# Retention and FFN on one core: the order of work in block 0's FFN, one tile's home, the order of products, one search operation

## The chip, the cores and the metric

The kernel runs on one core of a Trainium2 chip. A core has five engines with an instruction queue each: TensorE (PE: matmuls, with its weight loads listed apart as PEld), VectorE (DVE), ScalarE (ACT), GpSimd (POOL) and SyncE (SP), which here only issues DMAs. They work from SBUF, a memory of 128 partitions, and from PSUM, where matmuls accumulate. The metric is device time in microseconds (us).

## The reference, cut to what matters

x is 4 sequences of 1024 tokens, 512 wide, all fp32. Two sublayers follow each other, each with a plain layer norm before it and after it:

```python
x = x + layernorm(retention(layernorm(x)))
x = x + layernorm(ffn(layernorm(x)))

def retention(x):
    q, v = x @ Wq.T, x @ Wv.T
    ret = scan(v)                      # state = lam * state + v, along a sequence; one lam per head of 32
    y = layernorm(q * ret) * gamma + beta
    return (y * silu(x @ Wg.T)) @ Wo.T

def ffn(x):
    # each weight is rounded to fp8 (e4m3) and used in fp32; each product is scaled per output column
    gate = silu(qmm(x, gate_w, gate_scale))      # 512 -> 1536
    up = qmm(x, up_w, up_scale)                  # 512 -> 1536
    return qmm(gate * up, down_w, down_scale)    # 1536 -> 512
```

## The kernel before, in words

**Tiling.** The 4096 tokens are 8 blocks of 512 (t = 0 to 7). The main loop goes over the blocks, and in a block over 12 steps i, one for each 128 columns of the FFN's inner width. A step of block t issues on PE `f.gate(i)` (8 matmuls into the PSUM tile pfg), parts of the retention of block t+1 (b in the code), `f.up(i)` (8 into pfu) and `f.down(i-2)` (8 into the sums pd). A step takes PE about 8.89 us. n is the retention of block t+2, whose layer norm and transposed input xnT are prepared meanwhile. pfg and pfu share a pool of two PSUM tiles, so that the matmuls of a gate need the tile that ACT read for the gate before; `f.fuse(i)` is DVE's product of gate and up (the operation gate<-pfu,us_sb,gate, called gate_i STT here), and ACT's cast of it to fp32r (fuse); `f.rest(i)` is DVE's subtraction that leaves the cast's error (the "lo" half). The down products use both halves, as gate and up use both halves of their input x1nT (`upper_of`: ACT's cast; `rest_of`: DVE's rest).

**Order.** Every engine executes its instructions in the order of the program: the wrapper `InOrder` passes each one through `keep_in_program_order`, and all instructions therefore carry its line, L74, in the profile. The order is written out by hand. A wait at the head of an engine's queue holds all that is behind it.

**Block 0.** The FFN weights are rounded to fp8's grid while the loop's block 0 already runs, in pieces of 128x1024: `rounds` issues DVE's parts (a bitwise and on scr, an addition scr+scr, a subtraction into gate_sb, up_sb or down_sb), `units` ACT's two operations on scr between them. The squares' weights get sums on DVE (`weight_sums`) that are stored to DRAM by SP (`keep_sums`).

**Block 1's retention**, in block 0's loop, is done with plain matmuls. Its layer norm over y sums on PE: `halves()` splits a sum into hi (ACT) and lo (DVE), `mean()` and `var()` multiply both by a constant matrix. `center_y()` is four DVE subtractions y-mu, four ACT squares, and three POOL additions sqsum<-sqsum,sq. `silu(c)` puts the gate g_c into a tile with the tag "sg", of which three exist and which the FFN's gates use too.

**Blocks 2 to 7's retention** (`FAST = 2`) computes v, q and g with seven products of half size each (Strassen's way, in Winograd's form), in the order of the list `order`. Product j takes one of four sums of xnT's quarters, made by POOL (`input_sums`, t_sums), and a weight piece that SP fetches into a ring of four (`fetch_weights`, w_ring). Products 1, 2, 3 and 5 accumulate in the PSUM tile bank_a (5 begins it anew), 6, 7 and 4 in bank_b:

```python
if j == 1:
    act.copy(p1, bank)                              # p1 is a slice of the tile mids
elif j == 6:
    dve.tensor_tensor(c12, bank, p1, ALU.add)
elif j == 7:
    dve.tensor_tensor(s167, bank, p1, ALU.add)
elif j == 2:
    self.take(k, 0, 0, bank)                        # v: two scans on DVE
```

The first three products of v for block t+2 are issued in step 11 of block t.

**x1n, the FFN's input.** The layer norm of block t+1's x1 is made per 128 tokens s in steps 8 to 11: x1n_s (`x1n_of`; ACT with a bias nb in blocks 0 and 1, DVE from block 2 on). For s = 0 to 2 `move_x1n` transposes it by way of DRAM: a DVE transpose into xs, four stores mxs<-xs and a load x1n<-mxs on SP's queue. For s = 3 `turn_x1n` transposes it on PE (pt<-ident,x1n). In block t >= 1, step 11 ACT's order is: cast of x1n_2, cast of fuse_11, copy of product 1 into mids, cast of x1nT from pt.

**The search.** In block 1 ACT looks through the rounded weights for one beyond fp8's range: `find_over` yields 24 operations seen<-... of 128x1536. The list `look` says how many are issued in each of the 12 steps; half of them (rounded down) come behind `f.gate`, the rest near the step's end.

Of the kernel before, what the change touches and what calls it, by code (L numbers as in the profile page):

```python
# [10 lines left out]
F32 = mybir.dt.float32  # L11
I32 = mybir.dt.int32
F32R = mybir.dt.float32r
F8 = mybir.dt.float8e4
# [3 lines left out]
P = 128  # L18
# [5 lines left out]
def retention_ffn_sandwich(  # L24
# [24 lines left out]
    TB = 512  # L49
# [8 lines left out]
    big = ctx.enter_context(tc.tile_pool(name="big", bufs=1))  # L58
    work = ctx.enter_context(tc.tile_pool(name="work", bufs=2))
# [6 lines left out]
    class InOrder:  # L66
# [9 lines left out]
    pe, dve, act, pool, sp = (  # L76
        InOrder(e) for e in (nc.tensor, nc.vector, nc.scalar, nc.gpsimd, nc.sync)
    )
# [131 lines left out]
    def units():  # L210

        while open_units:
            _, c = open_units.pop(0)
            act.activation(c, c, AF.Relu, bias=neg_low)
            act.activation(c, c, AF.Identity, scale=1.5 * 2.0**20, bias=low_unit)

    def rounds(n, now=True):
        for _ in range(n):
            next(rounding, None)
            if now:  # L220
                units()

    def find_over():


        k = 0
        for j in range(4):
            for w in (gate_sb, up_sb, down_sb):
                v = w[:, ts(j, NI // 4), :] if w is down_sb else w[:, :, ts(j, I // 4)]
                for sign in (1.0, -1.0):  # L230
                    tag = "ret" if k >= 16 else "xn"
                    seen = work.tile(list(v.shape), F8, tag=tag, name=f"seen_{k}", bufs=2 if k >= 16 else 1)
                    act.activation(
                        seen, v.bitcast(F32), AF.Relu, bias=neg_max, scale=sign,
                        accum_out=over[:, k : k + 1], saturate=False,
                    )
                    k += 1
                    yield

    search = find_over()  # L240

    def pass_over():
# [54 lines left out]
    def ps_tile(name, home="pa"):  # L297
        if home == "pa":
            pa_turn[0] = 1 - pa_turn[0]
            home = f"pa{pa_turn[0]}"  # L300
        elif home[:2] == "pa":
            pa_turn[0] = int(home[2])
        return homes[home].tile([P, TB], F32, tag=home, name=name)
# [7 lines left out]
    def turn_by_blocks(dst, src, tag, name):  # L311


        t = work.tile([P, NQ, NC, Q], F32, tag=tag, name=name)
        dve.transpose(t, src.rearrange("p (c a i) -> p a c i", c=NC, a=NQ))
        m = dram.tile([P, NQ, NC, Q], F32, tag="turn", name=f"m{name}", bufs=2)
        for b in range(NQ):
            sp.dma_start(
                m[:, b].rearrange("(a i) c j -> i a (c j)", a=NQ),
                t[ts(b, Q)].rearrange("i a c j -> i a (c j)"),  # L320
            )
        sp.dma_start(dst, m)

# [4 lines left out]

    FAST = 2
    H = TB // 2
    order = [("v", j) for j in (1, 6, 2, 7, 4, 5, 3)]
    order += [("q", j) for j in (1, 6, 2, 7, 4, 5, 3)]
    order += [("g", j) for j in (1, 2, 6, 7, 4, 5, 3)]
    banks = {"v": {1: 0, 6: 1, 5: 0}, "q": {1: 1, 6: 0, 5: 1}, "g": {1: 0, 6: 0, 5: 1}}
# [23 lines left out]
    def keep_sums(k):  # L360
        for j, t in made[k].items():
            operands[k][j] = dram.tile([P, 2, H], F32, tag=f"sum_{k}{j}", name=f"dsum_{k}{j}", bufs=1)
            sp.dma_start(operands[k][j], t)
# [12 lines left out]
    class Retention:  # L376
# [89 lines left out]
        def product(self):  # L466

            k, j = order[self.made]
            n = (self.t - FAST) * len(order) + self.made
            self.made += 1  # L470
            w = w_ring[:, n % RING]
            if j in (1, 6, 5):
                bank = ps_tile(f"p{k}{j}_{self.t}", f"pa{banks[k][j]}").rearrange("p (c f) -> p c f", c=2)
                if j == 6:
                    self.bank_b = bank
                else:
                    self.bank_a = bank
            bank = self.bank_b if j in (6, 7, 4) else self.bank_a
            for o in range(2):
                out_ = bank[:, o]  # L480
                if len(self.right[j].shape) == 4:
                    out_ = out_.rearrange("p (g j) -> p g j", j=Q)
                for c in range(2):
                    pe.matmul(
                        out_, w[:, c, ts(o, P)], self.right[j][:, c],
                        start=(j in (1, 6, 5) and o == 0 and c == 0), stop=True,
                        skip_group_check=True,
                    )
            fetch_weights()
            c12, p1, s167 = (mids[:, m] for m in (1, 2, 3))  # L490
            if j == 1:
                act.copy(p1, bank)
            elif j == 6:
# [4 lines that stand above are left out]
                self.take(k, 0, 0, bank)  # L498
            elif j == 4:
                dve.tensor_tensor(p1, bank, p1, ALU.add)  # L500
                self.take(k, 1, 0, p1)
            elif j == 5:
                dve.tensor_tensor(s167, bank, s167, ALU.add)
                self.take(k, 1, 1, s167)
            else:
                dve.tensor_tensor(c12, bank, c12, ALU.add)
                self.take(k, 0, 1, c12)
# [116 lines left out]

        def silu(self, c):
            home = big if self.t == 0 and c == 3 else work
            tag = "fuse" if home is big else "sg"
            self.g[c] = home.tile([P, TB], F32, tag=tag, name=f"g_{self.t}_{c}", bufs=3)
            act.activation(self.g[c], self.pg.pop(c), AF.Silu)

        def g_of(self, c, home="pa"):
# [43 lines left out]
        def x1_moments(self, s):  # L675
            self.mvo[s] = moments(self.xt[s])

        def x1n_of(self, s):
            self.center(self.x1n[s], self.xt[s], self.mvo.pop(s))

        def new_x1nT(self):

# [9 lines left out]
        def move_x1n(self, s):  # L692

            x1n = self.x1n.pop(s)
            dst = x1n.rearrange("p (b c j) -> p b c j", b=NQ, c=NC)
            turn_by_blocks(dst, x1n, "ret", f"xs1_{self.t}_{s}")
            self.pt[s] = dst.rearrange("p b c j -> p c b j")

        def part(self, h, s):
            part = self.x1nT[:, h, :, ts(s, P)]  # L700
# [173 lines left out]
    b = Retention(1)  # L874
# [105 lines left out]

    look = [5, 5, 4, 2, 0, 0, 0, 2, 2, 2, 2, 0]
    l = None
    for t in range(NB):
        f, n = Ffn(a), None
        fast = b is not None and b.fast
        for i in range(NI):
            if t > 0 and (t > 1 or i):
                (f if i else l).rest((i - 1) % NI)  # L990
            if t == 0 and i == 0:
                n = Retention(2)
# [29 lines left out]
            if t == 0 and 8 <= i < 11:  # L1022
                for _ in range(4):
                    next(adding)
                if i == 10:
                    keep_sums("g")
            f.gate(i)
            if t == 0 and i in (5, 6):
                n.norm_x(2 * i - 10, True)
                n.norm_x(2 * i - 9, True)  # L1030
            for _ in range(look[i] // 2 if t == 1 else 0):
                next(search)

            if fast and i in (0, 1, 2, 3, 4, 5, 6):
# [12 lines left out]
                b.q(i + 2, tokens=slice(None) if i else later)  # L1047
                b.y_of(i + 2)
            if b and not fast and i == 3:
                b.halves()  # L1050
                units()
                rounds(3, now=False)
                units()
                b.g_of(0)
                b.mean()
                b.center_y()
                n.stats(3)
                n.rstd()
                n.shift()
# [14 lines left out]
                b.o(i - 7)  # L1074
            if b and i == 8:
                b.new_x1nT()
            if b and i >= 8:
                b.x1n_of(i - 8)
            if b and 8 <= i < 11:
                b.move_x1n(i - 8)  # L1080
            if b and i >= 9:
                b.upper_of(i - 9)
            if b and 7 <= i <= 10:
                b.o_moments(i - 7)
            if n and i == 11:
                n.input_sums(1, 2, 3, 4)
            units()
            f.up(i)
            f.fuse(i)
            if t == 0 and i == 4:  # L1090
                b.rstd_y()
            if n and i == 11:
                n.product()
                if t:
                    b.turn_x1n(3, "pf")
                    b.upper_of(3)
            if t == 2 and i == 0:
                next(passing)
            if fast and i < 6:
# [19 lines left out]
            if t == 0:  # L1119
                if i < 8 and i != 3:  # L1120
                    rounds(3, now=False)
                f.rest(i)
                if i < 3:
                    n.stats(i)
            for _ in range((look[i] + 1) // 2 if t == 1 else 0):
                next(search)

            if l and not b and i in (4, 5):
# [33 lines left out]
                f.down(NI - 2)  # L1162

            if t == 0 and i == 11:
                b.turn_x1n(3, "pf")
                b.upper_of(3)
                b.rest_of(3)
# [9 lines left out]
                b.var()  # L1177
                b.rstd_y()
            if n and i == 11:
                n.products(2)  # L1180
            if n and t > 0 and i == 5:
                n.stats(0)
                n.stats(1)
# [8 lines left out]
            if b and i == 4 and 0 < t < NB - 2:  # L1192
                n = Retention(t + 2)
# [4 lines left out]
        l, a, b = f, b, n  # L1198
# [68 lines left out]
```

## Time and profile before

| | |
|---|---|
| median of 3 runs | 984.25 us (983.97 to 984.66) |
| the profiled execution's own time | 983.95 us |
| its span, first to last instruction | 982.1 us |
| mean granted TensorE clock | 0.998 |
| busy: PE, PEld, DVE, ACT, POOL | 963.9, 734.3, 663.3, 369.9, 266.7 us |
| DMA | 110.07 MB, mean 112 GB/s |
| block 0's loop ends, block 1's FFN begins | about 203.3 us after the span's start |

PE's busy share by stage, from the trace cut at the blocks' borders: 194.5 of the first 203.0 us, 117.1 of the next 118.0, then 99.9% and more until 886, and 87.7 of the last 96.1. In a line of the timeline the two numbers ahead are start and busy time in us, then come the engine, the line of the code, the operation, out<-in by the program's names, the shapes, how often it was done in a row, and in brackets the idle time ahead of it and what ended that. In the waits view a line has the waiting engine and operation, whom it waited for, the total in us, how many waits, and the longest.

### The profile page before, as it was taken

To read this page: it belongs to the slowest core of one execution; us is meant where nothing else is said; L and a number is where in the kernel's file an instruction comes from. 1 tells how busy PE (TensorE), PEld (TensorE's weight loads), DVE (VectorE), ACT (ScalarE), POOL (GpSimd) and SP (SyncE) were. 2 spreads that over 40 slices of the span, in tenths; PEclk is the share of its full clock that TensorE was granted. 3 is DMA by queue.
4 is the path that set the end of the run, shared out by engine and by line. 5 is a ranking of instruction groups with operands and counts; after the bars stand their busy time and mean duration, and the time that the engine had idled before them with its cause. 6 is when DMAs were issued, how large, how long until landed. Compare 5 with 4: busy or idle time off the path is not lost.

```text
span 982.1 us, 11265 instructions
## 1 busy us (share of the span) xinstructions
PE 963.9 (98%) x3950; PEld 734.3 (75%) x3950; DVE 663.3 (68%) x1019; ACT 369.9 (38%) x556; POOL 266.7 (27%) x346
## 2 busy tenths in 40 slices
PE   9999999989999999999999999999999999999996
PEld 7456656678876888678876788768887788877885
DVE  5996979655667667675686666766667765756445
ACT  3546655467645125221432215321152211512223
POOL 1405121412324033240513305133141322322020
PEclk9999999999999999999999999999999999999999
DMA  9311413752416426253243623245241542213021
GB/s 300 119 65 65 130 63 94 228 161 75 151 53 156 128 82 225 80 143 120 86 129 93 176 77 116 87 131 151 83 150 59 135 140 76 75 37 113 1 86 43
DMA packets 90936, 110.07 MB, mean 112 GB/s; under 512 B 8064, under 2 KB 55424, under 8 KB 90880
## 3 DMA queue, kind: packets, MB, share of 16 engines
q1 hardware_dynamic: 90016, 108.70, 36.5%
q8 instruction: 31, 0.51, 0.2%
q10 hardware_dynamic: 864, 0.66, 0.2%
q14 instruction: 25, 0.20, 0.1%
HBM read 76.56 MB, written 32.77 MB: 111 GB/s over the span
## 4 chain that ended last, share of the span: by engine, by line
PE 84%; DVE 7%; ACT 4%; POOL 2%; DMA 1%; issue 1%; SPq 0%; DVEq 0%; POOLq 0%; ACTq 0%
PE pfu L74 15%; PE pfg L74 15%; PE pd L74 15%; PE pq L74 10%; PE pv L74 10%; PE po L74 9%; PE pg L74 9%; DVE scr L74 1%; DVE st L74 1%; DVE gate L74 1%; PE idle L74 1%; DVE xs L74 1%; DVE fuse L74 1%; DMA xnT<-mx 1%; POOL sqsum L74 1%
## 5 line engine op out<-in xcount | busy, mean ns | idle before, releaser
L74 PE MATMUL pfu<-x1nT,up_sb 128*128 128x512 f32 x768 | 211.5, 417 | 0.3 <-DVE gate L74 0.3
L74 PE MATMUL pfg<-x1nT,gate_sb 128*128 128x512 f32 x768 | 195.4, 396 | 1.4 <-ACT gate L74 1.4
L74 PE MATMUL pd<-down_sb,fuse 128*128 128x512 f32 x720 | 186.5, 400 | 0.0
L74 PEld LDWEIGHTS pfu<-x1nT,up_sb 128*128 128x128 f32 x768 | 144.4, 188 | 43.0 <-issue 13.4
L74 PEld LDWEIGHTS pfg<-x1nT,gate_sb 128*128 128x128 f32 x768 | 144.2, 188 | 31.7 <-ACT gate L74 1.8
L74 PEld LDWEIGHTS pd<-down_sb,fuse 128*128 128x128 f32 x720 | 134.9, 188 | 27.4
L74 ACT CAST fuse<-gate 128x512 fp32r<-128x512 f32 x90 | 55.7, 618 | 235.5 <-DVE gate L74 235.5
L74 ACT ACTIVATE gate<-pfg,gs_sb 128x512 f32<-128x512 f32 x96 | 65.7, 685 | 193.0 <-PE pfg L74 192.9
L74 DVE SCALAR_TENSOR_TENSOR gate<-pfu,us_sb,gate 128x512 f32<-128x512 f32 x96 | 71.7, 747 | 72.3 <-PE pfu L74 69.8
L74 PE MATMUL po<-wo_sb,y 128*128 128x512 f32 x256 | 114.5, 592 | 0.0
L74 POOL TENSOR_SCALAR mv<-mv 128x1 f32<-128x1 f32 (+1 forms) x82 | 19.9, 243 | 299.0 <-DVE mv L74 298.0
L74 PEld LDWEIGHTS po<-wo_sb,y 128*128 128x128 f32 x256 | 48.2, 189 | 50.3 <-issue 46.3
L74 DVE TENSOR_TENSOR fuse<-gate,fuse 128x512 fp32r<-128x512 f32 x90 | 74.5, 827 | 12.1 <-ACT fuse L74 12.1
L74 POOL TENSOR_TENSOR ysum<-y 128x256 f32<-128x256 f32 (+1 forms) x14 | 14.0, 1000 | 189.9 <-DVE y L74 189.9
L74 POOL TENSOR_TENSOR x<-x,x1n 128x512 f32<-128x512 f32 x32 | 46.8, 1463 | 45.6 <-DVE x1n L74 36.7
L74 DVE BATCH_NORM_STATS2 st<-x 128x6 f32<-128x512 f32 x64 | 43.6, 681 | 13.7 <-POOL x L74 11.3
L74 POOL TENSOR_TENSOR mv<-mv,nhalf 128x1 f32<-128x1 f32 (+1 forms) x75 | 46.3, 617 | 6.2
L74 PE MATMUL pg<-t_sums,w_ring 128*128 128x256 f32 x192 | 45.6, 380 | 0.6 <-ACT mids L74 0.6
L74 PE MATMUL pv<-t_sums,w_ring 128*128 128x256 f32 x192 | 45.4, 379 | 0.8 <-POOL t_sums L74 0.8
L74 PE MATMUL pq<-t_sums,w_ring 128*128 128x256 f32 x192 | 45.3, 379 | 0.0
L74 PEld LDWEIGHTS pg<-t_sums,w_ring 128*128 128x128 f32 x192 | 35.9, 189 | 7.3 <-ACT mids L74 2.0
L74 PEld LDWEIGHTS pv<-t_sums,w_ring 128*128 128x128 f32 x192 | 36.2, 189 | 6.6 <-POOL t_sums L74 1.0
(150 smaller groups left out, 1337.3 us busy)
## 6 DMA issues: line engine op xcount, KB each, us to landing
kept<-x SPq DMA_DIRECT2D x32, 256.0 KB, 2.1
x<-kept SPq DMA_DIRECT2D x32, 256.0 KB, 4.1
x<-in_x SPq DMA_DIRECT2D x28, 256.0 KB, 4.1
out<-d SPq DMA_DIRECT2D x27, 256.0 KB, 2.0
xnT<-mx SPq DMA_DIRECT2D x24, 256.0 KB, 4.9
w_ring<-dsum_v SPq DMA_DIRECT2D x24, 256.0 KB, 2.7
w_ring<-dsum_q SPq DMA_DIRECT2D x24, 256.0 KB, 2.6
w_ring<-dsum_g SPq DMA_DIRECT2D x24, 256.0 KB, 2.7
```

Source lines behind the costliest of these rows:

```text
L74: return lambda *args, **kwargs: tc.keep_in_program_order(op(*args, **kwargs))
```

## The change

1. **Step 3 of block 0.** `halves()` for block 1's mean moves to the end of step 2, ahead of `f.rest(2)`; the statistics of x_2 move from the end of step 2 into step 3; `g_of(0)`, `mean()` and `center_y()` now stand ahead of `rounds(3)` and the second `units()`, which stood ahead of them.
2. **Home of g_0.** Block 1's first gate gets a tile with the tag "tok" (four tiles, used by token tiles) instead of "sg".
3. **Step 11 of block 0.** Product 1 comes ahead of `f.fuse`, product 2 directly behind the down products and product 6 behind the transposes of x1n_3 (before: product 1 behind fuse, then transposes, 6, 2). x1n_3 is centred on DVE instead of ACT. The copy of product 1 of block 2's v goes to a tile of its own, and on ACT ahead of the cast of fuse_11. `turn_by_blocks` returns its final load, so that in step 10 `keep_sums("g")` stands between the stores of x1n_2 and its load. SP's order there becomes: weights of v's products 1 and 2, four stores of x1n_2, four stores of weight sums, load of x1n_2, a store of x, weights of products 6 and 7 (before: weights 1 and 6, four sums, four stores, load, store of x, weights 2 and 7).
4. **Order of v's products**, for all of blocks 2 to 7: 1, 2, 6, 7, 4, 5, 3 instead of 1, 6, 2, 7, 4, 5, 3. In step 11 of blocks 1 to 5 PE executes 1, transposes, down, 2, 6; ACT's order there stays.
5. **The search.** `look` becomes a list of pairs (behind the gate, at the end). One operation moves from the end of step 3 to the end of step 7 of block 1, and the 16th (k = 15) gets the tag "ret" instead of "xn".

The number of instructions stays the same on every engine.

```diff
--- before.py
+++ after.py
@@ -228,8 +228,8 @@
             for w in (gate_sb, up_sb, down_sb):
                 v = w[:, ts(j, NI // 4), :] if w is down_sb else w[:, :, ts(j, I // 4)]
                 for sign in (1.0, -1.0):
-                    tag = "ret" if k >= 16 else "xn"
-                    seen = work.tile(list(v.shape), F8, tag=tag, name=f"seen_{k}", bufs=2 if k >= 16 else 1)
+                    tag = "ret" if k >= 15 else "xn"
+                    seen = work.tile(list(v.shape), F8, tag=tag, name=f"seen_{k}", bufs=2 if k >= 15 else 1)
                     act.activation(
                         seen, v.bitcast(F32), AF.Relu, bias=neg_max, scale=sign,
                         accum_out=over[:, k : k + 1], saturate=False,
@@ -319,7 +319,7 @@
                 m[:, b].rearrange("(a i) c j -> i a (c j)", a=NQ),
                 t[ts(b, Q)].rearrange("i a c j -> i a (c j)"),
             )
-        sp.dma_start(dst, m)
+        return lambda: sp.dma_start(dst, m)
 
 
 
@@ -330,7 +330,7 @@
 
     FAST = 2
     H = TB // 2
-    order = [("v", j) for j in (1, 6, 2, 7, 4, 5, 3)]
+    order = [("v", j) for j in (1, 2, 6, 7, 4, 5, 3)]
     order += [("q", j) for j in (1, 6, 2, 7, 4, 5, 3)]
     order += [("g", j) for j in (1, 2, 6, 7, 4, 5, 3)]
     banks = {"v": {1: 0, 6: 1, 5: 0}, "q": {1: 1, 6: 0, 5: 1}, "g": {1: 0, 6: 0, 5: 1}}
@@ -488,6 +488,11 @@
                     )
             fetch_weights()
             c12, p1, s167 = (mids[:, m] for m in (1, 2, 3))
+            if k == "v" and self.t == FAST:
+
+                if j == 1:
+                    self.p1 = work.tile([P, 2, H], F32, tag="rstd", name="p1", bufs=1)
+                p1 = self.p1
             if j == 1:
                 act.copy(p1, bank)
             elif j == 6:
@@ -624,8 +629,8 @@
 
         def silu(self, c):
             home = big if self.t == 0 and c == 3 else work
-            tag = "fuse" if home is big else "sg"
-            self.g[c] = home.tile([P, TB], F32, tag=tag, name=f"g_{self.t}_{c}", bufs=3)
+            tag, bufs = ("fuse", 3) if home is big else ("tok", 4) if self.t == 1 and c == 0 else ("sg", 3)
+            self.g[c] = home.tile([P, TB], F32, tag=tag, name=f"g_{self.t}_{c}", bufs=bufs)
             act.activation(self.g[c], self.pg.pop(c), AF.Silu)
 
         def g_of(self, c, home="pa"):
@@ -675,8 +680,8 @@
         def x1_moments(self, s):
             self.mvo[s] = moments(self.xt[s])
 
-        def x1n_of(self, s):
-            self.center(self.x1n[s], self.xt[s], self.mvo.pop(s))
+        def x1n_of(self, s, center=None):
+            (center or self.center)(self.x1n[s], self.xt[s], self.mvo.pop(s))
 
         def new_x1nT(self):
 
@@ -693,8 +698,8 @@
 
             x1n = self.x1n.pop(s)
             dst = x1n.rearrange("p (b c j) -> p b c j", b=NQ, c=NC)
-            turn_by_blocks(dst, x1n, "ret", f"xs1_{self.t}_{s}")
             self.pt[s] = dst.rearrange("p b c j -> p c b j")
+            return turn_by_blocks(dst, x1n, "ret", f"xs1_{self.t}_{s}")
 
         def part(self, h, s):
             part = self.x1nT[:, h, :, ts(s, P)]
@@ -980,7 +985,7 @@
 
 
 
-    look = [5, 5, 4, 2, 0, 0, 0, 2, 2, 2, 2, 0]
+    look = [(2, 3), (2, 3), (2, 2), (1, 0)] + 3 * [(0, 0)] + [(1, 2)] + 3 * [(1, 1)] + [(0, 0)]
     l = None
     for t in range(NB):
         f, n = Ffn(a), None
@@ -1022,13 +1027,11 @@
             if t == 0 and 8 <= i < 11:
                 for _ in range(4):
                     next(adding)
-                if i == 10:
-                    keep_sums("g")
             f.gate(i)
             if t == 0 and i in (5, 6):
                 n.norm_x(2 * i - 10, True)
                 n.norm_x(2 * i - 9, True)
-            for _ in range(look[i] // 2 if t == 1 else 0):
+            for _ in range(look[i][0] if t == 1 else 0):
                 next(search)
 
             if fast and i in (0, 1, 2, 3, 4, 5, 6):
@@ -1047,13 +1050,13 @@
                 b.q(i + 2, tokens=slice(None) if i else later)
                 b.y_of(i + 2)
             if b and not fast and i == 3:
-                b.halves()
                 units()
-                rounds(3, now=False)
-                units()
+                n.stats(2)
                 b.g_of(0)
                 b.mean()
                 b.center_y()
+                rounds(3, now=False)
+                units()
                 n.stats(3)
                 n.rstd()
                 n.shift()
@@ -1074,26 +1077,35 @@
                 b.o(i - 7)
             if b and i == 8:
                 b.new_x1nT()
-            if b and i >= 8:
+            if b and i >= 8 and (t or i < 11):
                 b.x1n_of(i - 8)
             if b and 8 <= i < 11:
-                b.move_x1n(i - 8)
-            if b and i >= 9:
+                load = b.move_x1n(i - 8)
+                if t == 0 and i == 10:
+                    keep_sums("g")
+                load()
+            if b and i >= 9 and (t or i < 11):
                 b.upper_of(i - 9)
             if b and 7 <= i <= 10:
                 b.o_moments(i - 7)
-            if n and i == 11:
+            if n and t and i == 11:
                 n.input_sums(1, 2, 3, 4)
             units()
             f.up(i)
+            if t == 0 and i == 11:
+                n.input_sums()
+                n.product()
             f.fuse(i)
+            if t == 0 and i == 11:
+                b.x1n_of(3, center_scale)
+                n.input_sums(1, 2, 3, 4)
+                b.upper_of(2)
             if t == 0 and i == 4:
                 b.rstd_y()
-            if n and i == 11:
+            if n and t and i == 11:
                 n.product()
-                if t:
-                    b.turn_x1n(3, "pf")
-                    b.upper_of(3)
+                b.turn_x1n(3, "pf")
+                b.upper_of(3)
             if t == 2 and i == 0:
                 next(passing)
             if fast and i < 6:
@@ -1119,10 +1131,12 @@
             if t == 0:
                 if i < 8 and i != 3:
                     rounds(3, now=False)
+                if i == 2:
+                    b.halves()
                 f.rest(i)
-                if i < 3:
+                if i < 2:
                     n.stats(i)
-            for _ in range((look[i] + 1) // 2 if t == 1 else 0):
+            for _ in range(look[i][1] if t == 1 else 0):
                 next(search)
 
             if l and not b and i in (4, 5):
@@ -1162,6 +1176,7 @@
                 f.down(NI - 2)
 
             if t == 0 and i == 11:
+                n.product()
                 b.turn_x1n(3, "pf")
                 b.upper_of(3)
                 b.rest_of(3)
@@ -1177,7 +1192,7 @@
                 b.var()
                 b.rstd_y()
             if n and i == 11:
-                n.products(2)
+                n.products(2 if t else 1)
             if n and t > 0 and i == 5:
                 n.stats(0)
                 n.stats(1)
```

## The prediction

> **What bounds the kernel now.** I read the page's first and fourth parts, then TensorE's waits, then the timeline at each place that the diff touches.
>
> ```profile
> PE 963.9 (98%) x3950; PEld 734.3 (75%) x3950; DVE 663.3 (68%) x1019; ACT 369.9 (38%) x556; POOL 266.7 (27%) x346
> ...
> PE 84%; DVE 7%; ACT 4%; POOL 2%; DMA 1%; issue 1%; SPq 0%; DVEq 0%; POOLq 0%; ACTq 0%
> ```
>
> TensorE (PE) has work in 98% of the span, and the diff takes none of its matmuls away. So only stalls of PE count. Those of the waits view:
>
> ```profile
> PE pv L74 <- ACT x1nT L74: 1.4, 1, 1.4
> PE pfg L74 <- ACT gate L74: 1.4, 1, 1.4
> ...
> PE pv L74 <- POOL t_sums L74: 0.8, 1, 0.8
> PE pg L74 <- ACT mids L74: 0.6, 1, 0.6
> PE var L74 <- ACT half L74: 0.6, 1, 0.6
> PE mu L74 <- DVE half L74: 0.5, 1, 0.5
> PE pfu L74 <- DVE gate L74: 0.3, 1, 0.3
> ```
>
> A gap understates the loss, since matmuls overlap by about 0.16 us; I price a stall by the distance of starts, less the same distance undisturbed. In order of time: mean pair at 118.43, 0.76; variance pair at 128.43, 1.24; gate_6 at 143.60, 1.56; up_11 at 190.50, 0.48; at the end of block 0, transposes at 196.84 0.81, product 6 at 198.25 0.91, product 2 at 201.66 1.58; product 6 of g at 252.96, 0.80; product 1 at 314.61, 0.45. Together 8.6 us; the diff aims at most of them.
>
> Three timelines carry the argument. Block 0, step 0, where DVE and POOL (GpSimd) both work from SBUF:
>
> ```profile
> 43.92 5.71 POOL L74 TENSOR_TENSOR sqsum<-sqsum,sq 128x512 f32<-128x512 f32 x3 [1.28 <-ACT sq L74]
> ...
> 44.29 1.98 DVE L74 TENSOR_TENSOR scr<-scr 128x1024 f32<-128x1024 f32 x1
> ...
> 46.30 2.18 DVE L74 TENSOR_TENSOR gate_sb<-scr 128x1024 fp32r<-128x1024 f32 x1
> ...
> 48.41 1.77 DVE L74 TENSOR_SCALAR scr<-scr 128x1024 int32<-128x1024 int32 x1
> ```
>
> Undisturbed, these DVE operations take 1.22, 1.22 and 0.69 (118.30 to 121.4), and a POOL add 1.27. Here they alternate, each waiting for the other. Step 5, ahead of gate_6:
>
> ```profile
> 141.57 1.28 ACT L74 ACT_TABLE_LOAD   x1 [6.49 <-DVE fuse L74]
> ...
> 142.86 0.69 ACT L74 ACTIVATE gate<-pfg,gs_sb 128x512 f32<-128x512 f32 x1
> ...
> 143.60 2.14 PE L74 MATMUL pfg<-x1nT,gate_sb 128*128 128x512 f32 x8 [1.41 <-ACT gate L74]
> ```
>
> gate_6's PSUM tile is free once ACT has read gate_5's; ACT waited 6.49 for DVE's fuse_4 at 141.5. And the end of block 2's FFN, step 11:
>
> ```profile
> 435.38 0.62 ACT L74 CAST x1nT<-x1n 128x512 fp32r<-128x512 f32 x1 [4.10 <-DMA x1n<-mxs]
> 435.90 0.62 ACT L74 CAST fuse<-gate 128x512 fp32r<-128x512 f32 x1
> ...
> 436.43 0.58 ACT L74 COPY mids<-pv 128x512 f32<-128x512 f32 x1
> ...
> 436.49 1.89 PE L74 MATMUL pv<-t_sums,w_ring 128*128 128x256 f32 x8
> ```
>
> The copy of product 1, done at 437.00, sits on ACT behind a cast that waits for a DMA. PE is at product 6 then and feels nothing.
>
> [...]
>
> **Part 1, step 3 of block 0.** DVE's order becomes half lo, fuse_2, statistics of x_2, y−mu ×4, then the three rounding operations, then x_3's statistics and gate_3. Half lo is done at about 117.0 instead of 118.38: the mean's stall goes, −0.76. Work now runs from 118.0 on PE. But y−mu ends at 120.8 instead of 123.76, so POOL's three squares' adds start at 120.4, not 123.4, and meet the rounding operations[...]. By the alternation of the fence (bitand ends 0.55 after the POOL add ahead of it, a two-input operation 1.07 after, POOL 1.13 after DVE): bitand ends 122.24, subtraction 124.46, third POOL add 125.6, rounded weight 126.67, gate_3 128.13, against 125.22 before. Behind gate_3 on ACT stand the cast of fuse_3, gate_4 and the variance's hi half, behind that DVE's lo half (0.7): var's second matmul at 130.68, up_4 at 131.02 instead of 129.50. Net **+1.52**. If the adds slip past without blocking, up_4 starts at 128.20: −1.30. Both ends stay in; I take the upper, as the same operations did it 75 us earlier.
>
> **Part 2, home for g_0.** In the built order the table load and gate_5 follow fuse_4's cast on ACT directly, without the wait for DVE. So gate_5 runs at about 138 instead of 142.86, and the 1.56 at 143.60 goes. With part 1: **−0.04** at gate_6. DVE's own 2.04 wait for ACT's rounding (147.69) goes too, so its chain runs 0.6 earlier from step 5; gate_10 then ends at 189.84, PE wants it at 189.97: up_11's stall goes, **−0.48**, with a margin of only 0.13 (lost: 0).
>
> **Part 3, step 11 of block 0.** PE: product 1 ahead of fuse's work, then down, product 2, transposes, product 6. DVE now centres x1n_3, which beside POOL's t_sums costs 1.48 (432.57: 1.47; 0.55 alone). SP (DMA queue) issues the weights of v1, v2 ahead of the mxs stores, so v2 is no longer late (before it landed at 201.53), and v6, v7 after x1n_2's load; v6 lands near 198.2. The copy of product 1 goes ahead of fuse_11 on ACT. What becomes last is DVE: x1n_3 to 196.53, fuse_11's lo to 198.22, the rest of x1nT and the two scans to 201.68; block 1's first matmul at about 201.5, not 203.27. Of this −1.8, 0.5 is counted: **−1.28**. With nothing late on DVE the three stalls would give −3.3; if v6's weights landed 1.3 later, 0.
>
> **Part 4, order 1, 2, 6 for v in all fast blocks.** In blocks 1 to 5's step 11 ACT's order is unchanged, but PE now needs the copy before product 2, which goes into the bank being copied. Copy's end plus 0.05, less the time that PE is free (the start of product 6 before):
> - 319.81 and 318.75: 1.1
> - 437.01 and 436.49: 0.6
> - 554.00 and 554.00: 0.05
> - 672.22 and 671.56: 0.7
> - 789.77 and 789.08: 0.75
>
> Sum **+3.26**. Nothing stands on the gain side: product 6 did not wait there. It is nothing if x1n_2 lands 1.1 earlier.
>
> **Part 5, search.** Taking the operation out of step 3 removes the 0.80 at 252.96 (the same place without a search, in block 2, shows none): **−0.80**. Put into step 7 it costs ACT 1.70 (seen's pitch; 207.80 less 206.10) ahead of xn_1 at 285.21, then DVE's transpose at 286.05, statistics, gate_8. DVE and ACT keep only about 0.1 us of slack per 8.89-us step here, and xnT's landing is already 0.45 late at 314.61: **+1.5**; 0 if a slack that I can't see takes it. Its new home ("ret" for "xn") makes no wait that I see: nothing.
>
> Sum: −0.04 −0.48 −1.28 −0.80 +1.5 +3.26 = **+2.16**. On the profiled execution's 983.95: 986.1. The median of the runs is 0.3 above that: **986.4**.
>
> **Rivals.**
> (a) [...] (step 3). For it: part of POOL's adds may start ahead while DVE reads mu from PSUM. Against: 43.92. Then block 1 begins 4.6 earlier: −4.6 −0.80 +1.5 +3.26 = −0.65, time **983.6**: not slower. It decides if gate_3 ends by 125.3.
> (b) *The copy is ready before product 2* in blocks 1 to 5, because x1n_2's load lands 1.1 earlier relative to PE: −1.1, **983.2**. Against: landings of 2.6 to 4.7 us, which the diff leaves alone there. (a) and (b) together: 980.3.
> (c) *The home does not free gate_5* (the change does not do what it says): a further wait holds ACT to 142.9 plus part 1's 1.5. +1.56 and up_11's 0.48 come back, nearly 0.5 more: **988.9**. Against: the built order.
> (d) *Step 11 gains nothing* because v6's weights, now fourth on SP's queue, land late: +1.3 to +2, **988**.
>
> **How the numbers follow.** Main case 0.46, (a) 0.16, (b) 0.10, both 0.08, (c) 0.08, (d) 0.12. A measurement tells 0.2%, 1.97 us, from nothing: 982.28 and 986.22. The main case stands on the upper bound; its own range, 985 to 987.5, gives 0.30 slower and 0.16 same. Slower: 0.30 + 0.08 + 0.12 = 0.50. Faster: both 0.08 and 0.04 out of (a) and (b): 0.12. Same: 0.38. The range leaves out "both" at one end and (c)'s and (d)'s upper parts at the other: 982.7 to 988.6. The likeliest is slower, by about the smallest amount that shows.
>
> **What would show it.** Step 3: POOL adds of 2.1 us beside rounding from 120.4, gate_3 at 127.4, var waiting over 3 us (right); adds of 1.27 and var under 1.5 (rival a). Gate_6 without a wait for ACT. Step 11: DVE ending last, pt and product 6 waiting for x1n and for DMA little. Blocks 1 to 5: product 2 waiting for ACT's copy, 0.5 to 1.1 in four of five. Product 1 of block 1 waiting near 2 us for xnT. I am wrong if block 1 starts before 199, if product 2 does not wait, or if the waits of PE sum to less than before.

## The result, and the profile after

The changed kernel takes **987.27 us** (median of 7, 986.48 to 988.26) against 984.24 (7, 983.36 to 984.66): a ratio of 1.0031, 95% interval 1.0019 to 1.0043, slower by 3.0 us. The forecast was 986.4, in a range of 982.7 to 988.6, with slower as the likeliest. Medians here are over all executions of a kernel, so a single outlier (one kernel below had one of 1236 us, another one of 5142) does not move them. The experiments were measured in three series, each with the kernel before beside it: its medians there are 984.73, 984.5 and 984.65.

The profiled execution took 987.57 us, its span is 985.7. Busy time by engine, and the shares of the chain that ended last, from its page:

```profile
PE 965.9 (98%) x3950; PEld 735.5 (75%) x3950; DVE 670.3 (68%) x1020; ACT 369.4 (37%) x553; POOL 268.4 (27%) x346
...
PE 82%; DVE 7%; DMA 5%; ACT 3%; POOL 1%; issue 1%; SPq 1%; ACTq 0%; DVEq 0%; POOLq 0%
```

TensorE has the same 3950 matmuls and 2.0 us more busy time; none of that is new work: matmuls at a lower clock count as busy for longer, as the eight below that show 3.45 at a granted clock of 0.50 and took 2.00 before. The counts of the other engines do change, other than I wrote above: DVE has one operation more and ACT three fewer, since the centring of x1n_3 moved and its two small bias operations went. Of DVE's 7.0 us more, the centring is 1.5 (1.50 at 196.48). Most of the rest is operations that took longer beside POOL, and show as busy while they do: 2.9 in the three of step 3 below, and 2.1 in two subtractions in step 11 (1.76 and 1.74 at 197.90 and 199.58, 0.69 and 0.68 before). TensorE's waits (total, number, longest):

```profile
PE var L74 <- ACT half L74: 2.9, 1, 2.9
PE pv L74 <- ACT mids L74: 1.8, 5, 0.7
...
PE pv L74 <- DMA xnT<-mx: 1.2, 1, 1.2
PE pv L74 <- DMA w_ring<-dsum_v: 1.1, 1, 1.1
```

Of the waits shown of before, those of gate_6 (1.4), up_11 (0.3), the mean (0.5) and g's product 6 (0.6) are gone. The variance now waits 2.9 instead of 0.6, and there are five waits for ACT's copy that did not exist. Steps 3 and 4 of block 0, first before and then after, from the timeline:

```profile
118.30 0.69 DVE L74 TENSOR_SCALAR scr<-scr 128x1024 int32<-128x1024 int32 x1
...
118.90 1.22 DVE L74 TENSOR_TENSOR scr<-scr,scr 128x1024 f32<-128x1024 f32 x1
...
120.15 1.22 DVE L74 TENSOR_TENSOR gate_sb<-scr,scr 128x1024 fp32r<-128x1024 f32 x1
...
123.38 4.35 POOL L74 TENSOR_TENSOR sqsum<-sqsum,sq 128x512 f32<-128x512 f32 x3 [15.00 <-ACT sq L74]
...
124.50 0.72 DVE L74 SCALAR_TENSOR_TENSOR gate<-pfu,us_sb,gate 128x512 f32<-128x512 f32 x1
...
128.43 0.50 PE L74 MATMUL var<-half,mean_r 128*128 128x512 f32 x1 [0.58 <-ACT half L74]
```

```profile
120.93 5.21 POOL L74 TENSOR_TENSOR sqsum<-sqsum,sq 128x512 f32<-128x512 f32 x3 [12.01 <-ACT sq L74]
121.24 1.53 DVE L74 TENSOR_SCALAR scr<-scr 128x1024 int32<-128x1024 int32 x1
...
122.69 2.32 DVE L74 TENSOR_TENSOR scr<-scr,scr 128x1024 f32<-128x1024 f32 x1
...
125.05 2.17 DVE L74 TENSOR_TENSOR gate_sb<-scr,scr 128x1024 fp32r<-128x1024 f32 x1
...
127.96 0.72 DVE L74 SCALAR_TENSOR_TENSOR gate<-pfu,us_sb,gate 128x512 f32<-128x512 f32 x1
...
130.48 0.50 PE L74 MATMUL var<-half,mean_r 128*128 128x512 f32 x1 [2.85 <-ACT half L74]
...
131.54 3.45 PE L74 MATMUL pfu<-x1nT,up_sb 128*128 128x512 f32 x8
```

DVE's bitwise and, addition and subtraction took 1.53, 2.32 and 2.17 (0.69, 1.22, 1.22 before), POOL's adds 5.21 (4.35), and gate_3 came at 127.96 (124.50). The last line was in no forecast: eight matmuls that took 2.00 before took 3.45. Spread over up_4 and the down products behind it, matmuls ran at 0.427 us each instead of 0.227 from 131.8 to 135.2. The profile's record of the clock that TensorE was granted reads 0.50 from 131.71 to 135.13, and full speed ahead of that and behind it.

The same places at gate_6 and at the end of block 2's FFN:

```profile
137.13 1.28 ACT L74 ACT_TABLE_LOAD   x1
...
138.82 0.69 ACT L74 ACTIVATE gate<-pfg,gs_sb 128x512 f32<-128x512 f32 x1 [0.41 <-PE pfg L74]
...
145.70 1.98 PE L74 MATMUL pfg<-x1nT,gate_sb 128*128 128x512 f32 x8
```

```profile
436.04 0.62 ACT L74 CAST x1nT<-x1n 128x512 fp32r<-128x512 f32 x1 [3.86 <-DMA x1n<-mxs]
...
437.08 0.58 ACT L74 COPY mids<-pv 128x512 f32<-128x512 f32 x1
...
437.71 1.99 PE L74 MATMUL pv<-xnT,w_ring 128*128 128x256 f32 x8 [0.16 <-ACT mids L74]
...
439.55 1.89 PE L74 MATMUL pv<-t_sums,w_ring 128*128 128x256 f32 x8
```

In the first, the table load no longer waits 6.49 us for DVE, gate_5 is done at 139.5 and gate_6 starts with no bracket. In the second, product 2 (now ahead of product 6) waits for the copy at 437.08, which stands behind a cast that waits for its DMA.

When each matmul starts, less when the same matmul started before, gives the ledger. What differs ahead of any changed instruction is left out: 0.53 in this execution, 0.18 of it because the clock rose to full speed later (at 5.42 us and not 5.04) and the rest at a weight that landed later. The last column is another execution of the same kernel, profiled with the experiments; there 0.75 is left out, as the clock rose at 6.95 us. The last row but one is the time from the last matmul's start to the end of the span, 9.20 us instead of 8.75:

| term (us) | forecast | changed kernel | the same, again |
|---|---|---|---|
| step 3: mean and variance | +1.52 | +1.52 | +1.50 |
| slow matmuls behind the variance | none | +1.57 | 0 |
| home, at gate_6 | -1.56 | -1.53 | -1.56 |
| from gate_6's first matmul to up_11 | -0.48 | -0.64 | -0.57 |
| end of block 0 | -1.28 | -2.02 | -1.42 |
| g's product 6 | -0.80 | -0.73 | -0.76 |
| search: product 1 waits for xnT | +1.5 | +0.84 | +0.90 |
| transposes behind it | none | +0.42 | +0.34 |
| product 2 in blocks 1 to 5 | +3.26 | +3.22 | +3.61 |
| behind the last matmul | none | +0.44 | +0.44 |
| sum | +2.16 | +3.09 | +2.48 |

### The profile page after: what moved, and what is told of

Same layout as the page of the kernel before. It is cut to its first block, busy times and chain, and to the rows that moved or that the text cites. A ratio compares the mean times of both kernels' runs of the same rounds, so it can differ in the third digit from the quotient of the medians.

```text
span 985.7 us, 11253 instructions
## 1 busy us (share of the span) xinstructions
PE 965.9 (98%) x3950; PEld 735.5 (75%) x3950; DVE 670.3 (68%) x1020; ACT 369.4 (37%) x553; POOL 268.4 (27%) x346
## 4 chain that ended last, share of the span: by engine, by line
PE 82%; DVE 7%; DMA 5%; ACT 3%; POOL 1%; issue 1%; SPq 1%; ACTq 0%; DVEq 0%; POOLq 0%
PE pfg L74 15%; PE pfu L74 15%; PE pd L74 13%; PE pq L74 10%; PE pg L74 9%; PE po L74 9%; PE pv L74 9%; DMA mxs<-xs 2%; DVE st L74 2%; DMA x1n<-mxs 1%; DVE scr L74 1%; SPq L74 1%; POOL mv L74 1%; DVE gate L74 1%; ACT seen L74 1%
## 5 line engine op out<-in xcount | busy, mean ns | idle before, releaser
L74 PEld LDWEIGHTS pd<-down_sb,fuse 128*128 128x128 f32 x720 | 135.2, 188 | 27.6
```

The costliest lines, as they stand in the source:

```text
L74: return lambda *args, **kwargs: tc.keep_in_program_order(op(*args, **kwargs))
```

## The experiments

**The changed kernel again** (no edit).

> The changed kernel once more, as the base for its neighbours: 987.3. In its profile the eight gate/up matmuls behind the second variance matmul (131.5 to 135) took 0.427 each instead of 0.227, 1.6 in all. Theory C (TensorE's clock falls to half after the 2.85 us wait at the variance, on a grid of its own): the slow matmuls come again behind that wait, more or fewer of them, from run to run. Theory O (the half rate was chance, or another engine's traffic): none here, and about 1.6 less.

Measured: 987.94 (5 executions, 987.19 to 990.0). Its profiled execution was the quickest of the five and has no slow matmuls, although the variance waits just as long:

```profile
130.68 0.50 PE L74 MATMUL var<-half,mean_r 128*128 128x512 f32 x1 [2.83 <-ACT half L74]
...
131.75 2.00 PE L74 MATMUL pfu<-x1nT,up_sb 128*128 128x512 f32 x8
```

So the slow matmuls come from execution to execution, as theory C allows. The record of the granted clock says what they are: here it stays at full speed from 6.95 us to the end of the matmuls. In the 13 profiles with such a record there are seven stretches at 0.50 inside the loop, in six profiles, and the slow matmuls stand in them: it is the clock, and not other traffic, that makes them slow. Each is 3.41 us long and begins a whole number of 3.413 us after the clock first rose in that execution (37 in each of the six, 58 for the second stretch of one), 0.3 to 1.9 us behind the end of a wait. That is theory C's grid; whether it is the wait that brings the half clock on is for the runs below.

**Rounding ahead of the centring again.**

```diff
                 units()
+                rounds(3, now=False)
+                units()
                 n.stats(2)
                 b.g_of(0)
                 b.mean()
                 b.center_y()
-                rounds(3, now=False)
-                units()
                 n.stats(3)
```

> Changed kernel, but in step 3 of block 0 the three rounding operations stand ahead of g_0, the mean and the centring again (the early lo half and all other parts stay). Theory P (DVE's rounding and POOL's adds block each other, and the long wait costs the clock too): the adds take 1.27 again, rounding 0.69, 1.22, 1.22; the variance waits about 0.6 + 0.6; no slow matmuls; 1.5 + 1.6 less: 984.2. Rival N (the loss of step 3 is elsewhere): no more than 0.5 less, 986.8.

Measured: 985.57 (21, 984.72 to 987.12), 2.4 less than the changed kernel in the same series. In the timeline POOL's adds are at their old length, now behind the rounding, and gate_3 comes soon:

```profile
123.79 4.35 POOL L74 TENSOR_TENSOR sqsum<-sqsum,sq 128x512 f32<-128x512 f32 x3 [15.01 <-ACT sq L74]
...
124.92 0.72 DVE L74 SCALAR_TENSOR_TENSOR gate<-pfu,us_sb,gate 128x512 f32<-128x512 f32 x1
...
128.84 0.50 PE L74 MATMUL var<-half,mean_r 128*128 128x512 f32 x1 [1.32 <-ACT half L74]
...
129.91 3.01 PE L74 MATMUL pfu<-x1nT,up_sb 128*128 128x512 f32 x8
```

Rival N falls: more than 0.5 came back. But a part of the expectation missed: slow matmuls stand here too (3.01 for eight, and again in the down products), behind a wait of 1.32, less than half as long. The variance waits longer than before (0.58) only because the mean no longer does.

**Without POOL's adds.** The variance of block 1 is made from the first quarter of its columns alone.

```diff
-                    pool.tensor_tensor(self.sum, self.sum, sq, ALU.add)
+                    if self.t != 1:
+                        pool.tensor_tensor(self.sum, self.sum, sq, ALU.add)
```

> Changed kernel without POOL's three additions of block 1's squares (the variance of block 1 is made from a quarter of its columns), the order of all else as changed. Theory P: rounding on DVE takes 0.69, 1.22, 1.22 although it stands behind the centring; gate_3 is done near 125.4 instead of 128.7, the variance waits under 0.6, no slow matmuls: 3 to 3.8 less, 983.5 to 984.3. Rival N (rounding behind the centring is late anyway, whatever POOL does): rounding stays at 1.5, 2.3, 2.2 and under 0.5 is gained.

Measured: 983.75 (13, 982.62 to 984.6), 4.2 less than the changed kernel. Same order on DVE as in the changed kernel, no POOL beside it:

```profile
121.70 0.69 DVE L74 TENSOR_SCALAR scr<-scr 128x1024 int32<-128x1024 int32 x1
122.31 1.22 DVE L74 TENSOR_TENSOR scr<-scr,scr 128x1024 f32<-128x1024 f32 x1
...
123.56 1.23 DVE L74 TENSOR_TENSOR gate_sb<-scr,scr 128x1024 fp32r<-128x1024 f32 x1
...
125.52 0.72 DVE L74 SCALAR_TENSOR_TENSOR gate<-pfu,us_sb,gate 128x512 f32<-128x512 f32 x1
...
128.04 0.50 PE L74 MATMUL var<-half,mean_r 128*128 128x512 f32 x1
129.10 2.00 PE L74 MATMUL pfu<-x1nT,up_sb 128*128 128x512 f32 x8
```

That settles step 3: with the adds gone and nothing moved, the three operations have their undisturbed times to 0.01 us, gate_3 is 2.4 earlier although this execution started 0.5 later, the variance has no bracket and no slow matmuls follow. The order as such costs nothing; POOL beside it does. The 4.2 is not the price of that alone, since the adds also went from the variance's own chain.

**Eleven matmuls on ready data inside the wait.**

```diff
             var = ps_tile(f"var_{self.t}", "pa1" if self.fast else "pa")
+            if self.t == 1:
+                for _ in range(11):
+                    pe.matmul(var, mean_r, self.by_filler, start=True, stop=True)
             self.average(var)
...
                 b.g_of(1)
+                b.by_filler = a.x1nT[:, 0, 0]
                 b.var()
```

> Changed kernel with eleven matmuls on ready data into the variance's own PSUM tile ahead of its two (which begin it anew), so that TensorE is busy for about 2.5 of the 2.85 us of the wait. The wait's end stays where ACT's hi half puts it. Theory C: no slow matmuls behind it, 1.6 less where the changed kernel shows them: 985.7. Theory O: the slow matmuls stay or have nothing to do with the wait: 987.3.

Measured: 986.71 (15, 986.06 to 987.09), 1.2 less than the changed kernel in the same series, whose five executions (from 987.19 up) all lie above these 15; against the seven executions of the result (987.27) it is 0.6.

```profile
126.67 3.12 PE L74 MATMUL var<-x1nT,mean_r 128*128 128x512 f32 x11
130.05 0.50 PE L74 MATMUL var<-half,mean_r 128*128 128x512 f32 x1 [0.25 <-ACT half L74]
...
131.11 2.00 PE L74 MATMUL pfu<-x1nT,up_sb 128*128 128x512 f32 x8
```

The end of the wait did not move (the variance's first matmul is 1.5 later than before, the start's 0.14 taken off), TensorE did eleven useless matmuls more, and the kernel became faster: what was lost behind the wait was lost to idleness. That is for theory C. That 0.6 to 1.2 came back and not 1.6 fits slow matmuls in most executions but not all, and a part that the end of block 0 makes up; the runs do not tell these two apart.

**Order 1, 2, 6 for block 2 alone.**

```diff
-    order = [("v", j) for j in (1, 2, 6, 7, 4, 5, 3)]
+    order = [("v", j) for j in (1, 6, 2, 7, 4, 5, 3)]
...
+    first_order = [("v", j) for j in (1, 2, 6, 7, 4, 5, 3)] + order[7:]
...
-            k, j = order[n % len(order)]
+            k, j = (first_order if n < len(order) else order)[n % len(order)]
...
-            k, j = order[self.made]
+            k, j = (first_order if self.t == FAST else order)[self.made]
```

> Changed kernel with v's products in the order 1, 2, 6 for block 2 alone; blocks 3 to 7 have 1, 6, 2 again. Theory W (product 2 waits for ACT's copy in step 11 of blocks 1 to 5): all five waits go, 2.9 to 3.2 less than the changed kernel's 987.3 to 987.9: 984.5. Rival (the wait moves to product 6 or to the start of the next block): under 1 less.

Measured: 984.25 (13, 983.49 to 985.86), 3.0 less than the changed kernel's 987.27, with the kernel before at 984.5 in this series. The line of five waits for ACT's mids is gone from the waits view, and behind block 1's step 11 the starts keep their distance to before's to the end. Block 2's step 11:

```profile
435.61 0.86 PE L74 MATMUL pd<-down_sb,fuse 128*128 128x512 f32 x3
436.30 1.89 PE L74 MATMUL pv<-t_sums,w_ring 128*128 128x256 f32 x8
438.03 1.89 PE L74 MATMUL pv<-xnT,w_ring 128*128 128x256 f32 x8
439.57 2.20 PE L74 MATMUL pfg<-x1nT,gate_sb 128*128 128x512 f32 x8
```

No bracket: the wait moved nowhere. Theory W holds, at its size.

**The search divided as before.**

```diff
-                    tag = "ret" if k >= 15 else "xn"
+                    tag = "ret" if k >= 16 else "xn"
...
-    look = [(2, 3), (2, 3), (2, 2), (1, 0)] + 3 * [(0, 0)] + [(1, 2)] + 3 * [(1, 1)] + [(0, 0)]
+    look = [(2, 3), (2, 3), (2, 2), (1, 1)] + 3 * [(0, 0)] + [(1, 1)] + 3 * [(1, 1)] + [(0, 0)]
```

> Changed kernel with the search's operations divided as before (one at the end of step 3, one at the end of step 7 of block 1). Theory S: the wait of g's product 6 comes back (+0.7), product 1's wait for xnT falls from 1.2 to 0.3 (-0.8 to -0.9), and the wait for x1n_3 behind it (-0.3): 0.4 less, 987.1. Rival (xnT is late because TensorE came earlier, not because of the search): +0.7, 988.2.

Measured: 986.76 (13), against 987.27 and 987.94 for the changed kernel in other series: 0.5 to 1.2 less. The ratios to the kernel before, 1.0021 (1.0012 to 1.0029) against 1.0031 (1.0019 to 1.0043), overlap, so the medians alone do not show the gain.

```profile
PE pg L74 <- ACT mids L74: 0.6, 1, 0.6
```

g's product 6 waits again, the wait for xnT has left the list (product 1 is 0.18 late, 0.45 before), the one for x1n_3 stays at 0.26. The trace shows theory S's two waits change places; the rival would have cost 0.7.

**g_0 in an sg tile again.**

```diff
-            tag, bufs = ("fuse", 3) if home is big else ("tok", 4) if self.t == 1 and c == 0 else ("sg", 3)
+            tag, bufs = ("fuse", 3) if home is big else ("sg", 3)
```

> Changed kernel with g_0 in an sg tile again. Theory H (the home alone frees gate_5): gate_6 waits for ACT again, 1.5 to 2 more than the changed kernel: 989.2. Rival (the new order of step 3 had freed it): no change, 987.6.

Measured: 989.15 (5, 988.54 to 989.58), 1.2 to 1.9 more than the changed kernel. ACT's wait is back:

```profile
143.90 1.28 ACT L74 ACT_TABLE_LOAD   x1 [6.49 <-DVE fuse L74]
...
145.19 0.69 ACT L74 ACTIVATE gate<-pfg,gs_sb 128x512 f32<-128x512 f32 x1
```

In this execution, though, TensorE reaches gate_6 only at 145.97, since slow matmuls made it late by as much; the loss shows further on, as up_11's wait for DVE (0.3) and a gain at the end of block 0 of 1.46 instead of 2.66 from gate_6 on. Theory H holds in size; the place differs in an execution with slow matmuls.

**The home alone, on the kernel before.** The same line and `bufs`, nothing else.

> The kernel before with the home of g_0 alone. Gate_6 doesn't wait (-1.56), up_11 doesn't (-0.5); step 11 of block 0 may take some of it back, since its chain on DVE, POOL and the DMA queue does not come earlier by as much: 982.2 if nothing is taken, 983.5 if half is; rival (the home frees nothing without the new order of step 3): 984.3.

Measured: 982.28 (10, 981.61 to 983.0), ratio 0.9974 (0.9966 to 0.9983). In the trace gate_6 is 1.46 earlier, up_11 2.02, block 1 begins 1.8 earlier and the end of that block's FFN 1.57: 0.2 of the 2.02 is taken back at the end of block 0, and 0.45 by the end of block 1's FFN. The home does not need the rest of the change.

**Parts 1, 2 and 5 without step 11's.** The kernel before with the edits of step 3, the home and the search.

> The kernel before with parts 1, 2 and 5 alone: step 11 of block 0 and the order of the products stay as before. Its neighbour is the changed kernel with order 1, 2, 6 for block 2 alone (984.3). If part 3 was worth the 1.3 of my sum, 985.6; if it was worth the 2.0 that one trace showed, 986.3; if its gain was only that TensorE's slow matmuls were made up for there, 984.5.

Measured: 985.33 (14, 983.33 to 987.83). Its neighbour, measured in another series, is at 984.25 (13), so part 3 is worth about 1.1. The ratios to the kernel before, 1.0011 (1.0002 to 1.002) and 0.9999 (0.9991 to 1.0007), overlap: that there is a gain is likely, and 1.3 is not told from 2.0. In this trace the time behind the last matmul is 8.75, as in the kernel before, and in the neighbour's 9.20: the 0.44 of the ledger comes with what sets these two apart, step 11 of block 0 and block 2's order. Product 2 waited 2.13 at the end of block 0 here, and matmuls behind that wait were slow as well:

```profile
203.33 1.30 PE L74 MATMUL pv<-xnT,w_ring 128*128 128x256 f32 x3 [2.13 <-ACT x1nT L74]
```

**Four changes that the runs speak for.** To the changed kernel: rounding ahead of the centring and order 1, 2, 6 for block 2 alone, as above, and

```diff
-    look = [(2, 3), (2, 3), (2, 2), (1, 0)] + 3 * [(0, 0)] + [(1, 2)] + 3 * [(1, 1)] + [(0, 0)]
+    look = [(2, 3), (2, 3), (2, 2), (1, 0)] + 3 * [(0, 0)] + 4 * [(1, 1)] + [(1, 0)]
...
             if t == 0 and i in (9, 10):
-                for _ in range(RING // 2):
+                for _ in range(3 if i == 9 else 1):
                     fetch_weights()
```

> What the runs speak for: the changed kernel with rounding ahead of the centring again, order 1, 2, 6 for block 2 alone, the search's moved operation in step 11 of block 1 (behind gate_11, where ACT has 5 us free) instead of step 7, and the weights of product 6 fetched in step 9 with those of 1 and 2. From the run with the rounding moved back, 985.6: -2.9 for the order, -0.8 to -1.2 for the search, -0.8 for the weights: 981.0. If the gains hide behind each other (DVE's end of step 11, the landing of xnT): 982.5.

> The version of four changes once more, for its trace and on another set of runs: 981.0. Of TensorE's waits in it there should be left: the variance (about 1.3 + 0.2), at most 1 at the end of block 0, product 1 of block 1's step 11 about 0.3, and no wait for ACT's copy. If the slow matmuls come behind the variance's wait, 1.6 of the span are theirs.

Measured: 981.04 and 980.63 (5 each), ratios 0.996 (0.9947 to 0.9974) and 0.9959 (0.9947 to 0.9971): 3.5 to 4.0 us faster than the kernel before. The waits of the second run, and DVE at the end of block 0:

```profile
PE pfg L74 <- DVE x1nT L74: 1.8, 1, 1.8
...
PE var L74 <- ACT half L74: 1.4, 1, 1.4
```

```profile
195.87 1.75 DVE L74 TENSOR_TENSOR fuse<-gate,fuse 128x512 fp32r<-128x512 f32 x1
...
197.79 1.51 DVE L74 TENSOR_TENSOR x1nT<-x1n,x1nT 128x512 fp32r<-128x512 f32 x1 [0.17 <-ACT x1nT L74]
...
199.23 1.25 DVE L74 TENSOR_TENSOR_SCAN y<-lam,pv 128x256 f32<-128x256 f32 x2
200.40 0.66 DVE L74 TENSOR_TENSOR x1nT<-pt,x1nT 128x512 fp32r<-128x512 f32 x1
...
201.12 1.86 PE L74 MATMUL pfg<-x1nT,gate_sb 128*128 128x512 f32 x7 [1.76 <-DVE x1nT L74]
```

With the weights in time, DVE ends block 0: two subtractions of 0.69 take 1.75 and 1.51 beside POOL's t_sums. The expectation of at most 1 us there missed by 0.8. The searches in step 11 of block 1 cost no wait.

**The same with five matmuls ahead of the variance.** The edit is that of the eleven, with `range(5)`.

> The version of four changes with five matmuls on ready data ahead of the variance, as in the kernel with eleven. Theory C (a wait of 1.3 is enough to lower the clock in most executions): no slow matmuls, 0.6 to 1.2 less than without them on the same chip, and a narrower spread. Theory O (only the wait near 3 us does it): no difference within 0.3.

Measured: 980.52 (5) against 980.63 in the same series, no difference. Neither profile has slow matmuls, although the variance waits 1.4 + 0.2 without the five. Theory C in its stronger form, that 1.3 is enough in most executions, is not borne out: of the two profiles with that wait, one has slow matmuls and one does not.

## Why the prediction was right, and where it was not

The time lies 0.9 above the forecast and the mechanism is the one forecast, part by part. Two terms were missing, and some sizes offset each other.

- **Step 3, right.** The alternation was priced from the rows of step 0, and gate_3's delay and the variance's +1.52 came out to 0.02 in two executions. Rival (a), that the adds slip past the rounding, falls; the run without adds shows that POOL's adds beside the rounding are the cause: 1.53, 2.32 and 2.17 with them, 0.69, 1.22 and 1.23 without. One reading was wrong on the way: the operation called a subtraction at 124.46 is the addition. As for y-mu beside POOL, the adds of before began at 123.38, and only the last of the four y-mu (123.08 to 123.76) overlaps one of them, at an undisturbed 0.68.
- **Behind the variance, a missing step.** "Work now runs from 118.0 on PE" and a sum of starts treat a wait as lost time alone. Behind a wait of 2.8 us, 3.41 us of matmuls also ran at half clock: 1.57 in the first trace. It came in five of the six profiles with such a wait, and in neither of the two where it was filled or gone. Its price in the medians is the 0.6 to 1.2 of the run with eleven matmuls; part of the 1.57 is made up at the end of block 0, where chains on DVE and the DMA queue that had not been delayed were waiting. A wait of 1.32 us and one of 2.13 had a half clock behind them too. I had read the wait of over 3 us in my own forecast and not asked what it does to the clock.
- **Behind the last matmul, a second missing step.** In the changed kernel the last store is issued 6.16 us behind the last matmul's start, as before, but lands at 8.36 instead of 7.92. From the last matmul's start to the end of the span it is 9.18 to 9.24 us in all ten profiles of the changed kernel and of those built on it (that of the 5142-us execution left aside), and 8.75 in all three of the kernel before and of those built on it. Why the last stores land later was not settled.
- **Part 2, right**: -1.53 for -1.56 at gate_6, 0.16 more right behind its first matmul, and -0.48 for -0.48 at up_11, whose margin of 0.13 held. Rival (c) falls.
- **Part 3, right in size, partly by other waits.** -1.42 without slow matmuls for -1.28; less the 0.44 at the very end, if that is part 3's, it is -0.98. I named DVE as last. In the first trace it was first the weights of product 6 (1.10, landing near 200.7 and not 198.2), in the repeat POOL's t_sums (1.7), in two others DVE; three chains end within a microsecond there. Rival (d)'s late weights did occur, without its size. The last kernel shows DVE alone behind them.
- **Part 4, right in sum, less so in pieces.** The forecast's five pieces add to 3.20, and not to 3.26. The five waits are 0.81, 0.33, 0.45, 0.70 and 0.32 by the distance of starts, 2.6 together, since x1n_2's landings moved by some tenths; the forecast had 1.1, 0.6, 0.05, 0.7, 0.75. The other 0.6 is 0.1 to 0.15 per block that no wait shows: from product 2's start to the next product 1.84 instead of 1.73 at 437.71. Rival (b) falls.
- **Part 5, the sign right and the size not.** Product 1's wait cost 0.84 and not 1.5, with 0.42 more at the transposes behind it. More slack in the chain behind xn_1 than the 0.1 per step that I read would explain it; no run tests that. Putting the search back changed little over half a microsecond, as the two halves of the part nearly cancel.

The repeat, which had no slow matmuls, sums to 2.04 without the last row but one, where the forecast had 2.16. That it comes so close is in part luck: product 1's wait came out 0.60 lower than forecast, the transposes behind it 0.34 and product 2 0.35 higher. The medians differ by 3.0, which is 0.9 above the forecast's 2.16. The two missing terms are about the size of that miss: 0.44 behind the last matmul, and 0.6 by which the execution with slow matmuls exceeds the one without (3.09 and 2.48).

## What to carry to other kernels

When a change moves work on an engine, look at what then runs beside it: three DVE operations became 2.9 us longer beside POOL's three adds and were back at their old lengths in the run without those, and the rows that priced it stood elsewhere in the same trace. A reorder that helps one block should be restricted to that block: order 1, 2, 6 could stay for block 2, and cost 3 us over the other five. And a wait on TensorE like the 2.8 us here, which had 3.41 us of half clock behind it in five of six profiles, should be priced with that clock, or filled.

## What the runs showed of the hardware that I had not expected

- Half clock for 3.41 us, on a grid of 3.413 us that lies differently in each execution: behind waits of 2.8 us in five of six profiles, and behind 2 of the 14 waits of 1.3 to 2.2 us in all profiles (1.32 and 2.13). There was none where the wait was filled with useless matmuls, which made the kernel 0.6 to 1.2 us faster. What decides is not settled. TensorE was busy for 0.61 to 1.87 us of the grid's stretch ahead of the seven half clocks, but for 1.43 in a stretch of the repeat (126.41 to 129.83) with full speed behind it, so this share alone does not decide.
- The start of full speed lies differently in each execution too. The clock first rose to full speed between 4.02 and 7.26 us in the 13 profiles, and TensorE's matmuls on a constant at the start take 0.21 instead of 0.11 each until then; in the repeat they ended 0.91 later than before.
- With the wait filled, 15 executions lie within 1.0 us, where the changed kernel's five in the same series lie within 2.8. The wait is not the only source of such a spread: the kernel before, whose variance waits 0.58, has 43 within 4.5.
